# Full attention: steps spread over the beats, queries copied in another order, biases added by TensorE

## The chip, the cores and the metric

The kernel runs on one core of a Trainium2 chip. The metric is the device time of one execution in microseconds (us), the median of several runs. Engines are named as in the profile: PE (TensorE, matrix products), PEld (its weight loads), DVE (VectorE), ACT (ScalarE), POOL (GpSimd) and SP (SyncE, which here only issues transfers, DMAs). They run side by side, each through its own instructions in order, and wait for each other through semaphores.

## The reference, cut to what matters

```
x = L0_attn_x                                             # 16 batches, 512 tokens, 128 channels
x = x + _layernorm(windowed_attention(_layernorm(x)))     # stage 1
x = x + _layernorm(experts(_layernorm(x)))                # stage 2
x = x + _layernorm(full_attention(_layernorm(x)))         # stage 3, the one that is changed
x = x + _layernorm(sine_ffn(_layernorm(x)))               # stage 4

def full_attention(x):            # 16 heads of 8 channels
    qkv = x @ Wqkv + bqkv
    q, k, v = heads(qkv)
    q, k = rope(q), rope(k)
    attn = softmax(q @ k.T * 8 ** -0.5)                   # per batch and head, 512 x 512, no mask
    return merge(attn @ v) @ Wout + bout
```

All of it is computed in fp32. `_layernorm` here has neither gain nor bias.

## The kernel before

The four stages follow one another; `full_attention` is stage 3. Its instructions are recorded under `manual_schedule`: the order of the Python code is the order on each engine. A loop over *beats* writes that order out, 32 beats a batch (`BEATS`). An engine isn't tied to a beat: it goes on as soon as what it waits for is there.

**What each beat does.** `attend(b, k)` multiplies two tiles of scores (keys by queries, `sT`, L1104) and takes their exponentials on ACT (`ex`, L1110). `score(b + 1, k)` multiplies the scores of the next batch in the other order (`s`, L1070), of which DVE takes the greatest of each row (`nm`, L1073), since the softmax subtracts it. Three beats behind, every other beat, `products` multiplies four exponentials by the values (`po`, L1118), and every eighth beat `put_away` copies a finished tile out on ACT (`ou`, L1127) and writes it to DRAM (`heap`, L1128). Two score tiles (`two_banks`, also used by the transposes and projections), three `sT` tiles and one `po` tile fill PSUM.

**Tasks.** What a batch needs once is written as generators that `run_due` advances: `yield n` means that the next step is recorded n beats later. With beats counted from the first attend beat of a batch, modulo 32:

- `arrive` adds the experts' output to x: four gathers `hb` (POOL, L972), four scalings `y` (L978), the sum (L983), a norm, the sum with x (L986).
- `project` (two batches ahead of the attend beats) normalises x (`z_f`), transposes it (L995, ACT copy `zT` L997), multiplies queries and keys (`pqk`, L1002, ACT adds the bias, L1008) and values (`pv`, L1013; DVE adds their bias, L1017). POOL rotates queries and keys (three steps `t` for each half, L1029 to L1032). Each number is cut into a high part (`halves`, DVE, L964) and a rest (POOL, `cut`, L1035), which PE multiplies part by part. SP writes the parts to DRAM (`away`, L1038) and reads them back into the rows that PE needs (`qs`, `ks`, L1056): for each of two units z, queries and keys, two groups r and two parts i, so 16 transfers of 128 KB. Five tiles of queries and five of keys are used in turn.
- `greatest` transposes the greatest of each row (`pm`, L1081), cuts them (L1085) and writes four rows into the queries (L1090).
- `output` reads the heap back (`sc`, `oc`, L1135, L1137), inverts the sums (`rc`, L1140), spreads them over the channels by way of DRAM (`far`, `rb`, L1143, L1144), multiplies (`oT`, POOL, L1147), multiplies by Wout (`pf`, L1151), adds the bias on DVE (`fo`, L1153), normalises, and adds to x (L1156).

The norms (`normed_in`) are statistics on DVE (L182, L183), variance (L187), a power on POOL (L189), a product on DVE (L192) and four scalings on POOL (L197).

The biases of values and output lie in tiles of 128 equal rows:

```
vbias = wp.tile([P, 1, H1 * D1], F32, name="vbias")
bout = wp.tile([P, 1, C], F32, name="bout")
```

Of the kernel before, what the change touches and what calls it, by code (L numbers as in the profile page):

```python
# [20 lines left out]
F32 = mybir.dt.float32  # L21
# [851 lines left out]
def full_attention(net):  # L873
# [20 lines left out]
    with ExitStack() as ctx:  # L894
# [15 lines left out]
        for half in range(2):  # L910
# [8 lines left out]
        vbias = wp.tile([P, 1, H1 * D1], F32, name="vbias")  # L919
        nc.sync.dma_start(  # L920
            out=vbias[:, 0, :], in_=a["L1_attn_bqkv"].rearrange("(o n) -> o n", o=1)[:, 2 * C :].to_broadcast([P, C])
        )
        wo = wp.tile([P, C], F32, name="wo1")
        nc.sync.dma_start(out=wo, in_=a["L1_attn_Wout"])
        bout = wp.tile([P, 1, C], F32, name="bout")
        nc.sync.dma_start(
            out=bout[:, 0, :], in_=a["L1_attn_bout"].rearrange("(o c) -> o c", o=1).to_broadcast([P, C])
        )
        ones_row = net.ones[: H1, :]

        qs = [wp.tile([P, HQ, T], F32R, name=f"qs{i}") for i in range(5)]
        ks = [wp.tile([P, HQ, T], F32R, name=f"ks{i}") for i in range(5)]
        for i in range(5):
# [32 lines left out]
        def arrive(b):  # L966

            xb = net.x[b]
            hb = tok.tile([P, NTB, C], F32, name=f"hb_{b}", tag="fo")
            for j in range(NTB):  # L970
                n = b * NTB + j
                nc.gpsimd.indirect_dma_start(  # L972
                    out=hb[:, j, :], out_offset=None, in_=net.back,
                    in_offset=bass.IndirectOffsetOnAxis(ap=net.slots[:, n : n + 1], axis=0),
                )
            y = tok.tile([P, NTB, C], F32, name=f"y_{b}", tag="z")
            for j in range(NTB):
                nc.gpsimd.tensor_scalar(  # L978
                    y[:, j, :], xb[:, j, :], net.yr[:, b, j : j + 1], net.ynm[:, b, j : j + 1],
                    op0=ALU.mult, op1=ALU.add,  # L980
                )
            yield 11
            nc.gpsimd.tensor_tensor(y, y, hb, ALU.add)  # L983
            yield 4
            yield from normed_in(net, y, f"eo{b}", y)
            nc.gpsimd.tensor_tensor(xb, xb, y, ALU.add)  # L986

        def project(b):

            z = tok.tile([P, NTB, C], F32, name=f"z_f{b}", tag="z")  # L990
            yield from normed_in(net, net.x[b], f"f{b}", z)
            yield 3
# [31 lines left out]
            cuts = []  # L1024
            for half in range(3):

                if half < 2:
                    t1 = rp.tile([P, T], F32, name=f"t1_{b}_{half}", tag=f"t1{half}")
                    nc.gpsimd.tensor_tensor(t1, side[half], rope[:, 0, :], ALU.mult)  # L1029
                    t2 = rp.tile([P, T], F32, name=f"t2_{b}_{half}", tag="t2")  # L1030
                    nc.gpsimd.tensor_tensor(t2, side[1 - half], rope[:, 1, :], ALU.mult)  # L1031
                    nc.gpsimd.tensor_tensor(t1, t1, t2, ALU.add if half else ALU.subtract)  # L1032
                if half:
                    cut, t = cuts[-1]
                    nc.gpsimd.tensor_tensor(cut[:, 1, :], t, cut[:, 0, :], ALU.subtract)  # L1035
                    yield 1
                    for i in range(2):
                        nc.sync.dma_start(  # L1038
                            out=away.rearrange("k r z p h n t -> (k r z) n p h t")[:, :, i, half - 1, :],
                            in_=cut[:, i, :],  # L1040
                        )
                if half < 2:
                    yield 3
                    cut = rp.tile([P, 2, T], F32, name=f"cut_{b}_{half}", tag=f"cut{half}")
                    halves(cut[:, 0, :], t1)
                    cuts.append((cut, t1))
            yield 2
            for z in range(2):
                for kind, to in enumerate((qs, ks)):
                    for r in range(2):  # L1050

                        of = away[kind, r, z].rearrange("p h (d s) t -> p (h d) (s t)", s=HQ)
                        for i in range(2):
                            at = 64 * r + 2 * D1 * i
                            part = of[i : i + 1].to_broadcast([2, D1, HQ * T]) if kind == 0 else of
                            nc.sync.dma_start(  # L1056
                                out=to[(2 * b + z) % 5][at : at + 2 * D1, :, :].bitcast(F32), in_=part
                            )
                yield 3

        def score(b, k):

            z, s, i = k // (HQ * NTB), k // NTB % HQ, k % NTB
            q, kk = qs[(2 * b + z) % 5], ks[(2 * b + z) % 5]
# [10 lines left out]
        def greatest(b, z):  # L1075
# [6 lines left out]
            hi = rp.tile([P, P], F32, name=f"hi_m{b}_{z}", tag="hi_m")  # L1082
            halves(hi[:n], pm[:n, :P])
            lo = rp.tile([P, P], F32, name=f"lo_m{b}_{z}", tag="lo_m")
            nc.vector.tensor_tensor(lo[:n], pm[:n, :P], hi[:n], ALU.subtract)  # L1085
            yield 1
            for r in range(2):
                for j, part in enumerate((hi, lo)):
                    at, of = 64 * r + KR + j, r * HQ * NTB
                    nc.sync.dma_start(  # L1090
                        out=qs[(2 * b + z) % 5][at : at + 1, :, :].bitcast(F32), in_=part[of : of + HQ * NTB, :]
                    )

        def attend(b, k):
# [4 lines left out]
            q, kk = qs[(2 * b + s // HQ) % 5], ks[(2 * b + s // HQ) % 5]  # L1099
# [30 lines left out]
        def output(b):  # L1130
# [14 lines left out]
            yield 6  # L1145
# [4 lines left out]
            for j in range(NTB):  # L1150
                nc.tensor.matmul(pf[:, j, :], lhsT=oT[:, j * P : (j + 1) * P], rhs=wo, start=True, stop=True)  # L1151
            o = tok.tile([P, NTB, C], F32, name=f"fo_{b}", tag="fo")
            nc.vector.tensor_tensor(o, pf, bout.to_broadcast([P, NTB, C]), ALU.add)  # L1153
            yield 1
            yield from normed_in(net, o, f"fo{b}", o)
# [184 lines left out]
```

## Time and profile before

| what | value |
|---|---|
| time, median of 9 runs (lowest to highest) | 2858.79 us (2856.0 to 2874.71) |
| the profiled execution, its own time | 2862.25 us |
| its span, first to last instruction | 2860.5 us |
| mean granted TensorE clock | 0.841 |
| first and last attend beat (sT, L1104) | 1617.0 and 2637.5 us |
| DMA over the attend stage | 28% of 16 engines, 74 GB/s |

In the profile "busy" is time in which an engine works on an instruction. A wait is put down to what ended it. Rows of a timeline give the start, the time, the engine, the line, the operation, the tiles (out<-in) and, in brackets, the idle time before and what ended it. Rows of windows give the stretch, its length, then busy us and instructions of each engine, the granted TensorE clock (1.00 is full speed), the busy share of the DMA engines and GB/s.

### The profile page before, as it was taken

The page shows a single profiled execution, that of the slowest core. Times are in us where ns is not written, and L with a number is a line of the kernel's source. Part 1 is how long each engine was busy: PE and PEld are TensorE (multiplying, and loading weights), DVE is VectorE, ACT ScalarE, POOL GpSimd, SP SyncE. Part 2 cuts the span into 40 slices and gives each one's busy share as a digit, 9 for nine tenths or more (in the row PEclk, how much of TensorE's full clock was granted, in tenths as well). Part 3 has the DMA queues.
Part 4 walks back from the last instruction along what each step waited for, and adds up shares of the span by engine and source line. Part 5 has one row for each costly group of instructions (what it writes and reads, how often), then busy time and mean ns, then how long its engine had stood idle before and what let it go on. Part 6 is the DMA issues. An engine that isn't in the chain of part 4 may idle for free. (4 is left out here: it accounts for less than half of the span.)

```text
span 2860.5 us, 54880 instructions
## 1 busy us (share of the span) xinstructions
PE 2234.4 (78%) x21335; PEld 1263.0 (44%) x21335; DVE 1866.1 (65%) x3711; ACT 1389.2 (49%) x3176; POOL 1410.2 (49%) x1399
## 2 busy tenths in 40 slices
PE   5888988888889882377781698788888888898686
PEld 2555655555556551266770233333333333332354
DVE  3677777777777753856411667677667777771676
ACT  1445554555455450232330156556555555565676
POOL 2556656565665546333324335444444444410598
PEclk8999999999999995566795569889888888876898
DMA  6555555555555531011122223223223323220001
GB/s 173 168 169 151 168 158 161 160 166 160 161 152 164 161 112 51 14 33 39 47 57 48 53 71 84 77 80 85 75 79 83 85 79 80 79 62 29 21 23 33
DMA packets 164289, 275.45 MB, mean 96 GB/s; under 512 B 20419, under 2 KB 64957, under 8 KB 158909
## 3 DMA queue, kind: packets, MB, share of 16 engines
q1 hardware_dynamic: 157696, 259.41, 32.0%
q0 software_dynamic: 4096, 8.40, 1.2%
q10 hardware_dynamic: 2236, 4.12, 0.5%
q8 instruction: 169, 2.77, 0.4%
q14 instruction: 92, 0.75, 0.1%
HBM read 133.55 MB, written 114.03 MB: 87 GB/s over the span
## 5 line engine op out<-in xcount | busy, mean ns | idle before, releaser
L1073 DVE TENSOR_REDUCE nm<-s 128x2 f32<-128x1024 f32 x512 | 612.6, 1220 | 201.3 <-PE s L1070 168.3
L1110 ACT ACTIVATE ex<-sT 128x512 f32<-128x512 f32 x1024 | 537.9, 602 | 394.3 <-PE sT L1104 392.5
L380 POOL TENSOR_TENSOR t<-t,t 128x512 f32<-128x512 f32 x256 | 319.7, 1269 | 379.2 <-DVE t L377 328.4
L431 ACT ACTIVATE pr<-s,nmax 128x96 f32<-128x96 f32 x1024 | 250.8, 355 | 328.3 <-DVE nmax L425 323.2
L1104 PE MATMUL sT<-qs,ks 50*128 50x512 f32 x1024 | 373.2, 548 | 36.0 <-ACT ex L1110 35.9
L1070 PE MATMUL s<-ks,qs 48*128 48x512 f32 x1024 | 315.6, 500 | 89.7 <-DMA ks<-away 64.2
L1118 PE MATMUL po<-ex,vs 128*32 128x512 f32 x2048 | 335.8, 735 | 0.0
L1104 PEld LDWEIGHTS sT<-qs,ks 50*128 50x128 f32 x1024 | 150.7, 211 | 384.2 <-ACT ex L1110 252.3
L371 PE MATMUL pq<-xnT,wqk 128*128 128x512 f32 x512 | 264.4, 640 | 24.6 <-DVE t L377 23.4
L375 DVE TENSOR_TENSOR t<-pq,rope 128x1024 f32<-128x1024 f32 x128 | 156.5, 1223 | 167.8 <-DMA far<-t 89.5
L443 POOL TENSOR_TENSOR pr<-pr,rc 128x768 f32<-128x768 f32 x128 | 187.9, 1468 | 54.7 <-DVE rc L442 45.8
L1070 PEld LDWEIGHTS s<-ks,qs 48*128 48x128 f32 x1024 | 137.9, 220 | 129.8 <-issue 74.6
L456 ACT COPY prT<-pt 96x512 f32<-96x512 f32 x256 | 138.7, 602 | 111.5 <-PE pt L454 111.5
L392 PE MATMUL pv<-wv,xnT 128*128 128x512 f32 x256 | 151.5, 677 | 29.6 <-ACT v_odd L396 29.6
L377 DVE TENSOR_TENSOR t<-pq,rope 128x1024 f32<-128x1024 f32 x128 | 155.3, 1213 | 0.0
L454 PE MATMUL pt<-ident,pr 64*96 64x64 f32 x2048 | 84.6, 223 | 83.0 <-POOL pr L443 82.8
L425 DVE TENSOR_REDUCE nmax<-s 128x8 f32<-128x768 f32 x128 | 118.1, 923 | 46.4 <-PE s L420 46.3
L485 PE MATMUL pf<-wo,oT 128*128 128x128 f32 x1024 | 129.8, 281 | 15.1 <-ACT v_odd L396 15.1
L371 PEld LDWEIGHTS pq<-xnT,wqk 128*128 128x128 f32 x512 | 90.1, 196 | 112.3 <-issue 95.1
L485 PEld LDWEIGHTS pf<-wo,oT 128*128 128x128 f32 x1024 | 123.1, 194 | 32.8 <-ACT v_odd L396 17.3
L471 PEld LDWEIGHTS po<-prT,v_even 96*64 96x64 f32 x2048 | 103.3, 137 | 75.5 <-issue 39.4
L471 PE MATMUL po<-prT,v_even 96*64 96x64 f32 x2048 | 132.6, 228 | 0.7 <-ACT prT L456 0.7
(258 smaller groups left out, 4113.0 us busy)
## 6 DMA issues: line engine op xcount, KB each, us to landing
far<-t SPq DMA_DIRECT2D x256, 256.0 KB
kT<-far SPq DMA_DIRECT2D x64, 512.0 KB
qT<-far SPq DMA_DIRECT2D x64, 512.0 KB
away<-cut SPq DMA_DIRECT2D x64, 256.0 KB
qs<-away SPq DMA_DIRECT2D x128, 128.0 KB
ks<-away SPq DMA_DIRECT2D x128, 128.0 KB
heap<-ou SPq DMA_DIRECT2D x64, 256.0 KB
v_even<-v_odd SPq DMA_DIRECT2D x32, 384.0 KB
```

The costliest lines, as they stand in the source:

```text
L371: nc.tensor.matmul(ps[:, s], lhsT=wqk[:, kind, 2 * half + g, s, :], rhs=xnT[b][:, :T], start=True, stop=True)
L375: nc.vector.tensor_tensor(t1, ps, rope[:, 0:1, :].to_broadcast([P, 2, T]), ALU.mult)
L380: nc.gpsimd.tensor_tensor(t1[:, s], t1[:, s], t2[:, 1 - s], ALU.add if s else ALU.subtract)
L431: nc.scalar.activation(pr[:, r, j, :], s[:, r, j * KW : (j + 1) * KW], AF.Exp, bias=nmax[:, r, j : j + 1])
L443: nc.gpsimd.tensor_tensor(pr, pr, per_token(rc, KW), ALU.mult)
L471: nc.tensor.matmul(po[D0 * r : D0 * r + D0, t : t + 64], lhsT=v[:KW, j, at : at + D0], rhs=prT[:KW, c, r, j, :], start=True, stop=True,)
L485: nc.tensor.matmul(pf[:, i, :], lhsT=o[:, p, j * P : (j + 1) * P], rhs=wo[:, NP * half + p, :], start=(p == 0), stop=(p == NP - 1),)
L1070: nc.tensor.matmul(ps[:, r, :], lhsT=q[rows, s, i * P : (i + 1) * P], rhs=kk[rows, s, :], start=True, stop=True)
L1073: nc.vector.tensor_reduce(nms[b, z][:, :, s, i], ps, AX.X, ALU.max, negate=True)
L1104: nc.tensor.matmul(t, lhsT=kk[rows, s % HQ, i * P : (i + 1) * P], rhs=q[rows, s % HQ, :], start=True, stop=True)
L1110: nc.scalar.activation(e, st[r], AF.Exp, scale=SCALE1)
L1118: nc.tensor.matmul(outs[-1][PADH * j : PADH * (j + 1), :], lhsT=vs[b % 3][:, i, VW * (NJ * g + j) : VW * (NJ * g + j) + PADH], rhs=weights ...
```

## The change

It touches the full attention alone (and one helper, by an argument that is zero elsewhere). The steps of the tasks get other beats; the scores of a batch start 24 beats before its attend beats, not 32; projections and arrivals start earlier; each step by its beat, modulo 32:

| step | before | after |
|---|---|---|
| gathers hb | 10 (all four) | 7, 8, 9, 10 |
| scalings y; sum with hb | 10; 21 | 11; 16 |
| norm of arrive: statistics; power; scalings; x | 25, 26; 26; 28; 28 | 18, 19; 20; 22; 23 |
| norm of project: statistics; power; z_f | 0, 1; 1; 3 | 22, 23; 24; 26 |
| transposes; pqk; pv | 6; 8; 10 | 30; 0; 2 |
| rotation, first and second half | 10; 13 | 2; 5 |
| halves; cut | 13, 17; 13, 17 | 7, 10; 8, 11 |
| away | 14, 18 | 10, 13 |
| qs and ks of unit 0; of unit 1 | 20; 23 | 15; 20 |
| maxima of unit 0 (pm; rows) | 17; 18 | 25; 26 |
| maxima of unit 1 (pm; rows) | 1; 2 | 9; 10 |
| oT; pf | 14; 16 | 15; 17 |
| norm of output: statistics; power; scalings; x | 17, 18; 18; 20; 20 | 20, 21; 22; 24; 26 |

From the transposes to the units' copies, `project` stands in the batch two before its own in both kernels, with its norm in the batch three before in the changed one; its first score is at beat 0 of the next batch before, and at beat 8 after. Before the first attend beat the order changes too: arrival 1 comes before projection 0, and projection 1 before the first score.

The copies of queries: one transfer of 256 KB for each unit and group, in place of two of 128 KB, with 16 outer rows; the rows of queries and keys stand in another order, which leaves the sums alone. The biases of values and output are single rows, added by a further matmul with a row of ones; ACT then copies the PSUM tile, where DVE added the bias. Both parts of the maxima lie in one tile.

```diff
-def normed_in(net, x4, name, out, scale=None, mul=1.0, add=LN_EPS):
+def normed_in(net, x4, name, out, scale=None, mul=1.0, add=LN_EPS, apart=0):
...
     nc.vector.tensor_scalar(v, mv[:, :, 1], mul, add, op0=ALU.mult, op1=ALU.add)
+    if apart:
+        yield apart
     r = net.small.tile([P, k], F32, name=f"r_{name}", tag="cr")
...
+        vbias = wp.tile([1, C], F32, name="vbias")
+        bout = wp.tile([1, C], F32, name="bout")
...
                 nc.tensor.matmul(
                     pv[:, i, :], lhsT=zT[:, i * P : (i + 1) * P], rhs=raw[:, 2].rearrange("c h d -> c (h d)"),
-                    start=True, stop=True,
+                    start=True, stop=False,
                 )
-            nc.vector.tensor_tensor(
+                nc.tensor.matmul(pv[:, i, :], lhsT=net.ones[:1, :], rhs=vbias, start=False, stop=True)
+            nc.scalar.copy(
                 vs[b % 3][:, :, : VW * H1].rearrange("p i (h d) -> p i h d", d=VW)[:, :, :, :D1],
                 pv.rearrange("p i (h d) -> p i h d", d=D1),
-                vbias.to_broadcast([P, NTB, C]).rearrange("p i (h d) -> p i h d", d=D1),
-                ALU.add,
             )
...
                         of = away[kind, r, z].rearrange("p h (d s) t -> p (h d) (s t)", s=HQ)
+                        rows = to[(2 * b + z) % NH].bitcast(F32)
+                        if kind == 0:
+                            nc.sync.dma_start(
+                                out=rows[64 * r : 64 * r + 4 * D1, :, :],
+                                in_=of.rearrange("p d x -> (p d) x").unsqueeze(1).to_broadcast([2 * D1, 2, HQ * T]),
+                            )
+                            continue
                         for i in range(2):
                             at = 64 * r + 2 * D1 * i
-                            part = of[i : i + 1].to_broadcast([2, D1, HQ * T]) if kind == 0 else of
                             nc.sync.dma_start(
-                                out=to[(2 * b + z) % 5][at : at + 2 * D1, :, :].bitcast(F32), in_=part
+                                out=rows[at : at + 2 * D1, :, :], in_=of.rearrange("p d x -> d p x")
                             )
-                yield 3
+                yield 5
...
-                nc.tensor.matmul(pf[:, j, :], lhsT=oT[:, j * P : (j + 1) * P], rhs=wo, start=True, stop=True)
+                nc.tensor.matmul(pf[:, j, :], lhsT=oT[:, j * P : (j + 1) * P], rhs=wo, start=True, stop=False)
+                nc.tensor.matmul(pf[:, j, :], lhsT=net.ones[:1, :], rhs=bout, start=False, stop=True)
             o = tok.tile([P, NTB, C], F32, name=f"fo_{b}", tag="fo")
-            nc.vector.tensor_tensor(o, pf, bout.to_broadcast([P, NTB, C]), ALU.add)
-            yield 1
-            yield from normed_in(net, o, f"fo{b}", o)
+            nc.scalar.copy(o, pf)
+            yield 3
+            yield from normed_in(net, o, f"fo{b}", o, apart=1)
+            yield 2
...
+        LEAD = 24
+        arrivals = {(n - 4) * BEATS + 7: n for n in range(3, B)} | {-121: 0, -117: 1, -79: 2}
+        projections = {(n - 3) * BEATS + 22: n for n in range(1, B)} | {-100: 0}
         with tc.manual_schedule():
-            for beat in range(-3 * BEATS, (B + 1) * BEATS):
+            for beat in range(-4 * BEATS, (B + 1) * BEATS):
                 b, k = divmod(beat, BEATS)
+                sb, sk = divmod(beat + LEAD, BEATS)
...
-                if 0 <= b + 1 < B:
-                    score(b + 1, k)
-                    if k % (BEATS // 2) == BEATS // 2 - 1:
-                        tasks.append([beat, greatest(b + 1, 2 * k // BEATS)])
+                if 0 <= sb < B:
+                    score(sb, sk)
+                    if sk % (BEATS // 2) == BEATS // 2 - 1:
+                        tasks.append([beat, greatest(sb, 2 * sk // BEATS)])
...
-                if k == BEATS - 22 and b + 3 < B:
-                    tasks.append([beat, arrive(b + 3)])
-                if k == 0 and 0 <= b + 2 < B:
-                    tasks.append([beat, project(b + 2)])
+                if beat in arrivals:
+                    tasks.append([beat, arrive(arrivals[beat])])
+                if beat in projections:
+                    tasks.append([beat, project(projections[beat])])
```

More of the change, by code (lines that the diff above doesn't have):

```diff
@@ L918, in full_attention @@
                         )
[L919 to L922, printed above, removed]
+        vbias = wp.tile([1, C], F32, name="vbias")
+        nc.sync.dma_start(out=vbias, in_=a["L1_attn_bqkv"].rearrange("(o n) -> o n", o=1)[:, 2 * C :])
         wo = wp.tile([P, C], F32, name="wo1")
         nc.sync.dma_start(out=wo, in_=a["L1_attn_Wout"])
[L925 to L928, printed above, removed]
+        bout = wp.tile([1, C], F32, name="bout")
+        nc.sync.dma_start(out=bout, in_=a["L1_attn_bout"].rearrange("(o c) -> o c", o=1))
         ones_row = net.ones[: H1, :]
-        qs = [wp.tile([P, HQ, T], F32R, name=f"qs{i}") for i in range(5)]
-        ks = [wp.tile([P, HQ, T], F32R, name=f"ks{i}") for i in range(5)]
-        for i in range(5):
+        NH = 5
+        qs = [wp.tile([P, HQ, T], F32R, name=f"qs{i}") for i in range(NH)]
+        ks = [wp.tile([P, HQ, T], F32R, name=f"ks{i}") for i in range(NH)]
+        for i in range(NH):
             for r in range(2):
@@ L975, in arrive @@
                 )
+                yield 1
             y = tok.tile([P, NTB, C], F32, name=f"y_{b}", tag="z")
@@ L981, in arrive @@
                 )
-            yield 11
+            yield 5
             nc.gpsimd.tensor_tensor(y, y, hb, ALU.add)
-            yield 4
-            yield from normed_in(net, y, f"eo{b}", y)
+            yield 2
+            yield from normed_in(net, y, f"eo{b}", y, apart=1)
+            yield 1
             nc.gpsimd.tensor_tensor(xb, xb, y, ALU.add)
@@ L990, in project @@
             z = tok.tile([P, NTB, C], F32, name=f"z_f{b}", tag="z")
-            yield from normed_in(net, net.x[b], f"f{b}", z)
-            yield 3
+            yield from normed_in(net, net.x[b], f"f{b}", z, apart=1)
+            yield 4
             pz = two_banks(f"tp_f{b}")[:, 0, :]
@@ L1022, in project @@
             )
             away = dp.tile([2, 2, 2, 2, 2, HD * HQ, T], F32, name=f"away_{b}", tag="away")
[L1024 to L1035, printed above, removed]
-                    yield 1
[L1037 to L1046, printed above, removed]
@@ new lines, in project @@
+            ts = []
+            for half in range(2):
+                t1 = rp.tile([P, T], F32, name=f"t1_{b}_{half}", tag=f"t1{half}")
+                nc.gpsimd.tensor_tensor(t1, side[half], rope[:, 0, :], ALU.mult)
+                t2 = rp.tile([P, T], F32, name=f"t2_{b}_{half}", tag="t2")
+                nc.gpsimd.tensor_tensor(t2, side[1 - half], rope[:, 1, :], ALU.mult)
+                nc.gpsimd.tensor_tensor(t1, t1, t2, ALU.add if half else ALU.subtract)
+                ts.append(t1)
+                yield 3 - half
@@ new lines, in project @@
+            for half in range(2):
+                cut = rp.tile([P, 2, T], F32, name=f"cut_{b}_{half}", tag=f"cut{half}")
+                halves(cut[:, 0, :], ts[half])
+                yield 1
+                nc.gpsimd.tensor_tensor(cut[:, 1, :], ts[half], cut[:, 0, :], ALU.subtract)
+                yield 2
+                for i in range(2):
+                    nc.sync.dma_start(
+                        out=away.rearrange("k r z p h n t -> (k r z) n p h t")[:, :, i, half, :], in_=cut[:, i, :]
+                    )
@@ L1081, in greatest @@
             nc.tensor.transpose(pm[:n, :P], nm.rearrange("p r s i -> p (r s i)"), net.ident)
[L1082 to L1085, printed above, removed]
+            parts = rp.tile([P, P], F32, name=f"m{b}_{z}", tag="m")
+            halves(parts[:n], pm[:n, :P])
+            nc.vector.tensor_tensor(parts[64 : 64 + n], pm[:n, :P], parts[:n], ALU.subtract)
             yield 1
             for r in range(2):
-                for j, part in enumerate((hi, lo)):
-                    at, of = 64 * r + KR + j, r * HQ * NTB
+                for j in range(2):
+                    at, of = 64 * r + KR + j, 64 * j + r * HQ * NTB
                     nc.sync.dma_start(
-                        out=qs[(2 * b + z) % 5][at : at + 1, :, :].bitcast(F32), in_=part[of : of + HQ * NTB, :]
+                        out=qs[(2 * b + z) % NH][at : at + 1, :, :].bitcast(F32), in_=parts[of : of + HQ * NTB, :]
                     )
@@ L1098, in attend @@
             s = NJ // 2 * g + j
[L1099 removed]
+            q, kk = qs[(2 * b + s // HQ) % NH], ks[(2 * b + s // HQ) % NH]
             st = []
@@ L1144, in output @@
             nc.sync.dma_start(out=rb, in_=far.to_broadcast([H1, D1, T]))
-            yield 6
+            yield 7
             oT = op.tile([P, T], F32, name=f"oT1_{b}", tag="oT")
```

8 lines of the change are left out of this document (5 added, 3 removed).

## Prediction

> **What bounds the kernel now.** I read the page first, then the full attention by windows and by waits, then the timelines around its longest waits. The page:
>
> ```profile
> PE 2234.4 (78%) x21335; PEld 1263.0 (44%) x21335; DVE 1866.1 (65%) x3711; ACT 1389.2 (49%) x3176; POOL 1410.2 (49%) x1399
> PEclk8999999999999995566795569889888888876898
> ```
>
> TensorE is the busiest engine, and from the 15th slice on its granted clock is below full. The change touches only the full attention, whose attend beats run from 1617.0 (first sT, L1104) to 2638.9. The windows of that stage, then of three batches in it (us; busy us of PE, PEld, DVE, ACT, POOL; clock):
>
> ```profile
> 1617.00:2638.90 1021.90, 881.27 (x4397) 327.09 (x4397) 694.39 (x1036) 592.53 (x1129) 401.18 (x484) 0.82 0.28 74
> 1691.40:1756.90 65.50, 57.30 (x282) 21.40 (x280) 46.32 (x71) 37.32 (x72) 28.93 (x35) 0.79 0.24 69
> 1818.40:1879.60 61.20, 50.70 (x282) 19.30 (x282) 45.99 (x71) 37.13 (x72) 28.93 (x35) 0.92 0.32 85
> ```
>
> A batch takes 1021.9 / 16 = 63.9 us. DVE, ACT and POOL do the same work in both batches shown (46, 37, 29 us), and PE's busy time grows as its clock falls. No other engine fills a batch: PE, its clock and what it waits for set the pace. The windows of line 1104 alone (two matmuls a beat) give the pace at each clock:
>
> ```profile
> 1663.60:1690.50 26.90, 12.24 (x24) 5.37 (x24) 0.50 0.45 100
> 1824.00:1847.50 23.50, 8.90 (x28) 3.54 (x28) 1.00 0.29 94
> 1858.70:1879.00 20.30, 9.70 (x28) 3.89 (x28) 1.00 0.37 90
> ```
>
> At half clock a beat takes 26.9 / 12 = 2.24 us, at full clock 20.3 / 14 = 1.45 us, and 23.5 / 14 where the transposes and products of `project` lie among the beats. A mean clock of 0.82 means 36% of the stage at half clock. PE's waits in the stage and the two that recur in every batch:
>
> ```profile
> PE pf L1151 <- POOL oT L1147: 66.5, 12, 6.0
> PE s L1070 <- DMA ks<-away: 26.9, 15, 5.7
> 1792.52 2.08 PE L1151 MATMUL pf<-wo,oT 128*128 128x128 f32 x8 [5.28 <-POOL oT L1147]
> 1758.64 1.17 PE L1070 MATMUL s<-ks,qs 48*128 48x512 f32 x2 [1.82 <-DMA ks<-away]
> ```
>
> Beat 16 waits some 5.5 us for oT, beat 0 some 1.8 us for the queries and keys to be scored. After each the clock drops: 0.50 from 1759.3 to 1762.7 after the second one shown, and in other batches for 6.8 to 20 us. A wait of 1.13 us at 2520.7 was followed by 34 us at 0.50, in which PE was busy 34.1 of 34.1 us; gaps of 0.55 to 0.78 us (1838.6, 1777.3) were followed by none. So what must go are idle stretches from about 1.1 us up.
>
> Why oT is late, on POOL's timeline:
>
> ```profile
> 1775.54 1.27 POOL L1029 TENSOR_TENSOR t<-qk,rope 128x512 f32<-128x512 f32 x1 [6.80 <-ACT qk L1008]
> ...
> 1779.55 1.07 POOL L972 DMA_INDIRECT hb<-back,slots  x1 [0.16 <-issue]
> ...
> 1784.41 1.81 POOL L978 TENSOR_SCALAR y<-x,yr,ynm 128x128 f32<-128x128 f32 x4
> ...
> 1789.98 1.26 POOL L1035 TENSOR_TENSOR cut<-t,cut 128x512 f32<-128x512 f32 x1
> 1791.20 1.26 POOL L1147 TENSOR_TENSOR oT<-oc,rb 128x512 f32<-128x512 f32 x1
> ```
>
> POOL works without a gap from 1775.5 to 1792.5 on seven rotary and cutting steps (beats 10 and 13), four gathers and four scalings (beat 10); oT queues behind them. Batch 13, which has no arrival, has no such wait (pf began at 2496.27 without one). Why the queries are late, on SP's timeline:
>
> ```profile
> 1811.36 8.00 SPq L1056 DMA_DIRECT2D qs<-away  x4
> 1819.43 1.77 SPq L1056 DMA_DIRECT2D ks<-away  x4
> ```
>
> Four issues for queries take 8 us, each waiting for an earlier query transfer to land (2.45 us apart); four for keys take 1.8 us, and the score waits for them behind the queries.
>
> **The change, part by part.** *POOL spread.* From beat 2 POOL now does six rotary steps (6 x 1.26), four gathers (4 x 1.25), two cuts (2 x 1.26) and four scalings (1.8): 16.9 us. Starting when ACT's qk is out, some 3 us into the batch, and waiting about 2 us for DVE's halves of beat 7, it is through near 22 us. oT's input rb leaves SP after rc of beat 8 (about 17 us) and the 1.5 us that SP waited between far and rb (1776.99, 1778.46), so lands by about 22. oT ends near 23.5; PE comes to beat 17 at 17 x 1.45 + 3 = 27.6. The wait goes with 4 us to spare; if that cover fails it costs 5.5 us again and the clock.
>
> *Projection earlier.* The query transfers of unit 0 are issued 25 beats before their first score instead of 12, 36 us against 17. The wait of beat 0 goes even if the transfers gained nothing. The new form halves the query issues; SP has 32 DMAs a batch, not 36.
>
> The Trainium skill ("DMA: Bandwidth & Descriptors", section on why a DMA increments its semaphore by 16) states that the slowest dimension decides over how many of the 16 engines a transfer goes. By that rule queries go from 2 engines to 16, but keys, whose source now has 8 outer rows, from 16 to 8: it speaks against that part. The 8.0 and 1.8 us rows above agree with it for before; by the rule or without it the sum here is the same, as 36 us cover either.
>
> *Maxima later.* LEAD 24 puts the maxima of unit 1 on SP at beat 10, needed at beat 16. Ahead of them on SP stand rb, heap and two away, behind POOL's cut; four issues at 0.6 us. From rb at 19 us: heap 0.4, away 1.2, maxima 2.4, landing about 2, so 25 us against beat 16 at 26. That is thin.
>
> *Biases.* Eight matmuls a batch of two passes: in place of "pv" and "pf" with 8 passes there are 16 each. pf's 8 passes took 1.09 us at full clock (2496.27 to the next start at 2497.36). No one-row matmul is in the trace: from 0 (hidden under PE's waits for DVE) to 0.38 us each (the first, isolated pass of pv, 1839.15); I take the neighbours' 0.12: 16 x 0.12 = 1.9 us. DVE loses two additions of 0.69 us, ACT gains two copies of 0.59 us (rows of vs, fo and zT); ACT's 37 us leave room. Each copy waits for its matmuls, and behind it the next exponentials wait 0.6 us, inside PE's present gaps; PE would notice only through its three sT buffers.
>
> *DVE.* The statistics of three norms (four pairs of about 0.4 and two steps of 0.16 each, 1.9) now lie in beats 18 to 23: 5.7 us beside 6 x 1.22 of maxima, 12.9; PE has 6 x 1.45 + 2 of pf, 10.7. That overhang of some 2 us is mostly buffered by two score tiles; between 0 and 2, I take 0.4.
>
> *A batch then.* 32 x 1.45 = 46.4; project's extra 23.5 - 14 x 1.45 = 3.2; pf 1.1; biases 1.9; DVE 0.4: 53 us at full clock.
>
> *Start.* Arrival 1 now comes before projection 0, and projection 1 before the first score. POOL's work from the first gather (1503.57) to z of batch 1 is three arrivals of 12.1, one projection of 12.9 and 2.8: 52; with waits for DVE and ACT like those in its rows (2.0 x 2, 5.5) about 62, and 5.5 more to qk: first score at 1571.5, against 1565.8. Then 24 beats at (1617.0 - 1565.8) / 32 = 1.6 us: 1610, 7 earlier. The bounds are 1600 and 1625.
>
> *Sum.* Start 1610; batch 0, half clock for its first 3 beats, 55; batches 1 to 13 at 53, 689; batch 14 without projection 49; batch 15: 8 beats at 1.45, 10 alone at 1.30, 14 alone at 2.1 (as batch 15 did, half clock from its 12th beat), pf: 55. That ends at 2458; the tail of 2860.5 - 2638.9 = 222 stays: 2680, 1.8 around it as before (2862.25 against 2860.5): 2682. The median of the runs lies 3.5 below the profiled one: **2678 us**.
>
> The Trainium skill ("TensorE: Matmul & The Clock Gate", Part 1) says one busy window of 3.4 us brings full clock back. By this rule a batch would lose its two waits, 7.3 us, and twice 3.4 us at half clock, 2.4 us: less 1.9 for the biases that is 7.8 us, 117 in 15 batches, and with the start 7 the estimate would be 2735. The 34 us at 0.50 with PE fully busy contradict the rule, so the rows decide.
>
> **The rivals.** *oT stays late* (POOL's crowd is only moved): against it, batch 13; for it, rb or halves may hold POOL. Price: 5.5 us plus 6.8 us at half clock (2.5) a batch, 14 x 8 = 112: 2790. *The clock falls in beats 18 to 26*, where DVE holds PE: 9 beats of 0.8 us, 14 x 7 = 98: 2776. Against it, PE would still be busy 10.7 of 12.9 us there.
>
> *The maxima come late at beat 16*, the one that ends slower. If they land over 1.1 us after PE is there, it idles, and the clock stays low until the transposes of beat 30: 1.5 + 15 x 0.79 = 13.4 us on top of 53 is 66.4, above today's 63.9: 15 x 13.4 = 201, so 2879. For it, the 1 us of slack; against it, pf's matmuls stand at beat 17, and after today's late pf the clock came back within 6.8 us.
>
> *The change does not do what it says*: the order of the instructions on each engine shows the steps moved as described, and nothing before the attention; I give this nothing.
>
> **How the numbers follow.** Forecast 0.64, oT late 0.12, clock in the DVE stretch 0.14, maxima late 0.08, no net effect 0.02. The forecast's own range: start -10 to +15, biases -1.9 to +4 a batch (-27 to +60): 2640 to 2750. Reaching to the two mild rivals: 2640 to 2795. A change under 0.3%, 8.6 us, can't be told from none. Faster 0.90, same 0.02, slower 0.08.
>
> **What would show it.** Right: no wait of pf for oT or of s for ks over 1 us, clock near 1.0 from batch 1 to 14, batches of 51 to 55 us, first sT near 1610. Wrong: sT of beat 16 waiting for a DMA; half clock for ten beats in a batch; pf still in the waits; a 16-pass pf far above 2.2 us.

## The result, and the profile after

The changed kernel takes 3080.29 us (median of 20 runs, 3036.7 to 3110.28), the kernel before 2854.07 us in the same comparison: ratio 1.0758, 95% interval 1.0729 to 1.0786. It is slower by 7.6%, where 2678 us and faster was forecast. A ratio compares, of each kernel, only the executions within 1.5% of its fastest, so it can differ a little from the ratio of the medians. The profiled execution took 3068.59 us, with a span of 3066.8 us.

The page of the changed kernel, PE's busy time and the granted clock by slices:

```profile
PE 2570.8 (84%) x21591; PEld 1395.1 (45%) x21591; DVE 1863.7 (61%) x3679; ACT 1406.4 (46%) x3208; POOL 1411.7 (46%) x1399
PEclk8999999999999955778855755555755557575799
```

TensorE has 256 more matmul records than before, 1.2% of them, and 336 us more busy time. Nothing of that size was added; the slices with 5 say where it comes from. The windows of the attend stage, first sT (line 1107 here) to the last (start:end, length; busy us of PE, PEld, DVE, ACT, POOL; clock):

```profile
1614.60:2840.70 1226.10, 1205.11 (x4641) 453.54 (x4641) 694.78 (x994) 605.36 (x1157) 386.53 (x462) 0.60 0.22 61
```

The stage is 204.2 us longer than before (1021.9), the whole span 206.3. PE is busy 1205.1 of 1226.1 us, so it waits less than before, and its mean clock went from 0.82 to 0.60. PE's waits in the stage, all that the view lists:

```profile
PE sT L1107 <- ACT ex L1113: 12.2, 44, 0.8
PE s L1073 <- ACT zT L999: 3.3, 9, 0.7
PE sT L1107 <- DMA qs<-m: 3.3, 2, 1.8
PE pqk L1004 <- DVE nm L1076: 0.5, 1, 0.5
```

pf no longer waits for oT (66.5 us before), s no longer for ks (26.9 us). The waits that the change was to take away are gone, and the clock is lower all the same. The timeline of the values' product in one batch shows what TensorE does just before the clock falls (start, us, engine, line, operation, tiles, xcount):

```profile
1849.60 0.49 PE L1015 MATMUL pv<-raw,zT 128*128 128x128 f32 x2
1850.02 0.48 PE L1019 MATMUL pv<-vbias,ones 1*128 1x128 f32 x2
1850.43 0.49 PE L1015 MATMUL pv<-raw,zT 128*128 128x128 f32 x2
1850.85 0.48 PE L1019 MATMUL pv<-vbias,ones 1*128 1x128 f32 x2
...
1852.93 0.51 PE L1107 MATMUL sT<-qs,ks 50*128 50x512 f32 x2
```

The 16 passes take 1852.93 - 1849.60 = 3.33 us, 0.21 us each; without biases the 8 passes of this block took 1.09 us at full clock. The windows of that block, of the stretch after it, and of a pf block with the stretch after it:

```profile
1849.60:1852.93 3.33, 3.33 (x18) 2.36 (x17) 1.23 (x1) 1.25 (x3) 3.25 (x3) 1.00 0.21 79
1853.80:1861.00 7.20, 7.20 (x29) 2.35 (x21) 3.59 (x3) 3.17 (x7) 2.78 (x3) 0.50 0.17 46
2733.86:2737.18 3.32, 3.32 (x20) 2.36 (x16) 0.34 (x1) 0.00 (x0) 0.00 (x0) 1.00 0.00 0
2737.90:2843.70 105.80, 101.74 (x344) 32.40 (x341) 32.03 (x47) 51.50 (x100) 9.35 (x13) 0.50 0.07 22
```

In both blocks PE is busy without a gap at full clock, and within 1 us of their ends the clock is 0.50: the second time for 105.8 us, through the rest of the stage, in which PE was busy 101.7. A *fall* is from here on a change of the granted clock from 1.00 to 0.50. The traces show no other values, and in the attend stages the times between two changes are whole multiples of 3.41 us, so the 3.41 us ahead of a fall are the window to look at. Of the 19 falls in the stage, 17 follow a window with five to eight one-row passes and no idle time. The other two follow the wait for the maxima at beat 16 (1.78 and 1.48 us). In the kernel before, every fall followed a window in which PE was busy for at most 2.45 of 3.41 us.

### The profile page after: what moved, and what is told of

It reads as the page before. It is cut to its first block, busy times and chain, and to the rows that moved or that the text cites. A ratio compares the mean times of both kernels' runs of the same rounds, so it can differ in the third digit from the quotient of the medians.

```text
span 3066.8 us, 55235 instructions
## 1 busy us (share of the span) xinstructions
PE 2570.8 (84%) x21591; PEld 1395.1 (45%) x21591; DVE 1863.7 (61%) x3679; ACT 1406.4 (46%) x3208; POOL 1411.7 (46%) x1399
## 4 chain that ended last, share of the span: by engine, by line
PE 38%; POOL 4%; DVE 4%; ACT 3%; issue 1%; DMA 1%; POOLq 0%; ACTq 0%; DVEq 0%; SPq 0%
PE po L1121 13%; PE sT L1107 12%; PE s L1073 6%; DVE nm L1076 1%; PE pqk L1004 1%; PE pf L1154 1%; PE pf L1155 1%; ACT ex L1113 1%; PE pv L1019 1%; PE pv L1015 1%; POOL go L199 1%; POOL turns L1277 1%; POOL x L1300 1%; DVE whole L1281 1%; DMA qs<-m 1%
## 5 line engine op out<-in xcount | busy, mean ns | idle before, releaser
L1076 DVE TENSOR_REDUCE nm<-s 128x2 f32<-128x1024 f32 x512 | 621.5, 1220 | 450.0 <-PE s L1073 443.1
L1107 PE MATMUL sT<-qs,ks 50*128 50x512 f32 x1024 | 470.3, 684 | 17.6 <-ACT ex L1113 12.2
L1121 PE MATMUL po<-ex,vs 128*32 128x512 f32 x2048 | 441.9, 952 | 0.0
L1073 PE MATMUL s<-ks,qs 48*128 48x512 f32 x1024 | 411.6, 611 | 18.3 <-DVE nm L1076 14.7
L1107 PEld LDWEIGHTS sT<-qs,ks 50*128 50x128 f32 x1024 | 200.1, 267 | 486.3 <-issue 286.8
L1073 PEld LDWEIGHTS s<-ks,qs 48*128 48x128 f32 x1024 | 183.3, 285 | 35.6 <-DVE nm L1076 26.1
```

The lines of the kernel that those rows point to most:

```text
L1073: nc.tensor.matmul(ps[:, r, :], lhsT=q[rows, s, i * P : (i + 1) * P], rhs=kk[rows, s, :], start=True, stop=True)
L1076: nc.vector.tensor_reduce(nms[b, z][:, :, s, i], ps, AX.X, ALU.max, negate=True)
L1107: nc.tensor.matmul(t, lhsT=kk[rows, s % HQ, i * P : (i + 1) * P], rhs=q[rows, s % HQ, :], start=True, stop=True)
L1121: nc.tensor.matmul(outs[-1][PADH * j : PADH * (j + 1), :], lhsT=vs[b % 3][:, i, VW * (NJ * g + j) : VW * (NJ * g + j) + PADH], rhs=weights ...
```

## The experiments

Two theories were put first. **A**: a matmul over one row leaves the array nearly empty, so the clock gate takes a window full of them for an idle one. **B**: the harm is in the alternation of two sets of weights, whatever their rows. A third, **C**: the new places of the steps (LEAD, the longer pauses) are to blame, the biases are not. The runs fall into three comparisons, in which the kernel before took 2870.66, 2856.46 and 2852.19 us; each ratio is to the one of its own comparison.

**Biases back on VectorE, all else as changed.**

```diff
-  nc.tensor.matmul(pv[:, i, :], lhsT=net.ones[:1, :], rhs=vbias, start=False, stop=True)
-  nc.scalar.copy(vs..., pv...)
+  nc.vector.tensor_tensor(vs..., pv..., vbias..., ALU.add)      # and the same for pf, bout
```

> The changed kernel with the biases added by DVE again, as before; everything else stays changed. Theory A (the one-row matmuls let the clock fall: 16 of the 19 falls in the changed kernel's attend beats follow a window with 5 to 8 one-row passes and no idle time): the falls after pv and pf vanish, the stage is at full clock except after a late maxima row at beat 16; 2680 to 2850 us, mean clock over the attend stage above 0.8. Theory B (it is the alternation of one-row and full weights, 0.21 us a pass in place of 0.11, whatever the rows): the same as A. Theory C (the new places of the steps pull the clock down, the biases cost only their own 5 us a batch): about 3080 - 15 x 5 = 3000 us, clock in the stage still near 0.6.

Measured: 2768.33 us (2755.52 to 2783.59), ratio to the kernel before 0.9635 (0.9567 to 0.9702). The biases' form alone turns a gain of 3.6% into a loss of 7.6%; C falls. Stage and waits of this kernel:

```profile
1626.50:2559.20 932.70, 862.14 (x4409) 319.38 (x4409) 711.62 (x1023) 590.89 (x1128) 387.63 (x462) 0.85 0.29 80
PE s L1078 <- DVE nm L1081: 16.1, 27, 1.0
PE sT L1112 <- DMA qs<-m: 11.8, 13, 2.1
```

The stage lost 293.4 us against the changed kernel. What is left to explain is a batch of 58.3 us (932.7 / 16) where 53 was forecast. The clock still falls 21 times. Seven falls come 28 to 29 us into a batch, after waits of 0.83 to 2.08 us for the maxima at beat 16; one comes in the last batch, and the other 13 come 38 us or later into a batch, where PE waits for VectorE's score maxima. Six of these follow a single wait of 0.67 or 0.68 us, with the rest of the window almost all busy. One such wait and its window, after which the clock fell at 1797.42:

```profile
1796.37 0.50 PE L1078 MATMUL s<-ks,qs 48*128 48x512 f32 x2 [0.67 <-DVE nm L1081]
1794.01:1797.42 3.41, 2.71 (x20) 1.01 (x16) 3.23 (x12) 2.06 (x4) 0.40 (x2) 1.00 0.85 169
```

**The kernel before, with only the one-row biases and the copies by ScalarE.**

```diff
-  nc.vector.tensor_tensor(vs..., pv..., vbias..., ALU.add)
+  nc.tensor.matmul(pv[:, i, :], lhsT=net.ones[:1, :], rhs=vbias, start=False, stop=True)
+  nc.scalar.copy(vs..., pv...)                                   # and the same for pf, bout
```

> The kernel before with one part of the change alone: biases by one-row matmuls and copies on ACT, all steps at their old beats. Theories A and B: each pv at beat 10 and pf at beat 16 is followed by half clock; the attend stage is at half clock 70 to 80% of its time and the kernel takes 3000 to 3150 us. Theory C: only the time of the passes is added, 15 x 5 us: about 2930 us.

Measured: 2957.11 us (2944.79 to 2973.33), ratio 1.0326 (1.0257 to 1.0396). Same direction, less than expected: the time lies between C's 2930 us and the 3000 from which A and B start, and doesn't decide between them. The clock does: in the stage it went from 0.82 to 0.77, and 15 of its 27 falls now follow windows with six to eight one-row passes and less than 0.1 us without work. That the loss is smaller because the kernel before already ran much of its stage at half clock is likely, and was not tested.

**The bias matmuls over all 128 rows.**

```diff
-  vbias = wp.tile([1, C], F32)        # the bias, one row
+  vbias = wp.tile([P, C], F32)        # the bias / 128 in every row
-  nc.tensor.matmul(pv[:, i, :], lhsT=net.ones[:1, :], rhs=vbias, ...)
+  nc.tensor.matmul(pv[:, i, :], lhsT=net.ones, rhs=vbias, ...)   # and the same for pf
```

> The changed kernel with as many bias matmuls, but each over 128 rows (a tile of ones times 128 rows of a 128th of the bias) in place of one. Theory A (rows count): clock as in the kernel with DVE biases, plus 16 passes of 0.11 us a batch: within 60 us of that kernel, 2700 to 2880. Theory B (alternation of weights counts, or ACT's copies): passes still 0.21 us and the clock still falls after pv and pf: 3040 to 3100. Theory C: 3000 to 3080.

Measured: 2789.02 us (2769.22 to 2797.09), ratio 0.973 (0.9671 to 0.979). The number of matmuls and their alternation are those of the changed kernel; only the rows differ. Timeline of the values' block, and windows of the stage and of this block with 1.5 us behind it:

```profile
1872.46 0.49 PE L1019 MATMUL pv<-raw,zT 128*128 128x128 f32 x2
1872.78 0.39 PE L1023 MATMUL pv<-vbias,ones 128*128 128x128 f32 x2
1873.01 0.39 PE L1019 MATMUL pv<-raw,zT 128*128 128x128 f32 x2
...
1874.44 0.50 PE L1111 MATMUL sT<-qs,ks 50*128 50x512 f32 x2
```
```profile
1626.00:2546.00 920.00, 827.95 (x4641) 326.55 (x4642) 692.99 (x994) 603.12 (x1157) 387.68 (x462) 0.92 0.29 81
1872.46:1875.90 3.44, 3.44 (x29) 2.31 (x28) 1.90 (x2) 2.57 (x6) 3.36 (x4) 1.00 0.23 81
```

Sixteen passes take 1874.44 - 1872.46 = 1.98 us, about 0.12 each, the price that the prediction put on them, and no fall of the clock follows any of these blocks. B falls. A bias matmul on TensorE isn't what hurts; one with few rows is.

**One one-row matmul of 512 columns for each tile, ahead of the four products.**

```diff
+  nc.tensor.matmul(pv, lhsT=net.ones[:1, :], rhs=vbias.unsqueeze(1).to_broadcast([1, NTB, C]), start=True, stop=False)
   for i in range(NTB):
-      nc.tensor.matmul(pv[:, i, :], lhsT=zT..., rhs=raw..., start=True, stop=False)
-      nc.tensor.matmul(pv[:, i, :], lhsT=net.ones[:1, :], rhs=vbias, start=False, stop=True)
+      nc.tensor.matmul(pv[:, i, :], lhsT=zT..., rhs=raw..., start=False, stop=(i == NTB - 1))
```

> The changed kernel with one bias matmul of one row over all 512 columns of the tile, ahead of the four products, in place of four of 128 columns between them. The one-row passes go from 8 of 0.21 us, alternating, to 2 of about 0.22 to 0.43 us in one piece. Theory A: less than 1.1 us of nearly empty array, so falls after pv and pf become rare: 2700 to 2900 us. Theory B: no alternation, so the same. Theory C: about 3000 us. If a single one-row matmul is enough for a fall, the time stays above 3000 too and the half-clock stretches still begin right after pv and pf.

Measured: 2831.37 us (2788.99 to 2860.48, the widest spread here), ratio 0.9785 (0.968 to 0.9889). The block takes 2.14 us, and a single fall follows bias passes with no other gap beside them. Two readings stay open after this: few one-row columns (A), or few changes between one row and 128 (call it **D**, since such changes cost time, 3.33 against 1.98 us for 16 passes, and that time might be an idle array).

**32 rows.** Against the changed kernel:

```diff
-  vbias = wp.tile([1, C], F32)
+  vbias = wp.tile([32, C], F32)       # the bias / 32 in every row
-  nc.tensor.matmul(pv[:, i, :], lhsT=net.ones[:1, :], rhs=vbias, ...)
+  nc.tensor.matmul(pv[:, i, :], lhsT=net.ones[:32, :], rhs=vbias, ...)   # and the same for pf
```

> The changed kernel with each bias matmul over 32 rows (ones times a 32nd of the bias) in place of 1: between the changed kernel (one row, 3080 us) and e3 (128 rows, 2789). If the clock's gate weighs rows in proportion, 32 rows are a quarter of the array: most falls after pv and pf stay, 2950 to 3080. If any matmul that fills one group of 32 rows counts, 2770 to 2830. If weights that differ in rows can't be loaded beside each other (0.21 us a pass), that stays at 32 rows too, and shows apart from the clock.

Measured: 3035.84 us (3022.97 to 3054.06), ratio 1.0623 (1.0545 to 1.07). The blocks take 3.33 us again, and 19 of 20 falls follow them. So 32 rows hardly help, under A and D alike.

**64 rows**, the same with 64, and **one-row passes in a row**: the one-row matmul of 512 columns twice, with half the bias each, ahead of the products. The first keeps the changes of row count and doubles the rows; the second doubles the one-row time and has one change.

```diff
-  vbias = wp.tile([32, C], F32); lhsT=net.ones[:32, :]
+  vbias = wp.tile([64, C], F32); lhsT=net.ones[:64, :]           # the bias / 64; the same for pf
```
```diff
-  nc.tensor.matmul(pv, lhsT=net.ones[:1, :], rhs=vbias.unsqueeze(1)..., start=True, stop=False)
+  for half in range(2):               # vbias halved once at the start; the same for pf
+      nc.tensor.matmul(pv, lhsT=net.ones[:1, :], rhs=vbias.unsqueeze(1)..., start=half == 0, stop=False)
```

> The changed kernel with each bias matmul over 64 rows (ones x bias/64). Passes of 1 and of 32 rows that alternate with 128-row passes followed each other 0.21 us apart (16 passes in 3.33 us), passes of 128 rows 0.11 us apart (1.98 us). Two readings are left. Rows weigh (A): a 64-row pass counts half, the window's loss halves, few falls follow the bias blocks, 2790 to 2850. Each switch between a pass of fewer rows and one of 128 empties the array for 0.10 us (D): the block still takes 3.33 us, falls follow it as they do with 32 rows, 3010 to 3080.

> The kernel with one one-row matmul of 512 columns ahead of the four products (2831), but that matmul is there twice with half the bias each, so 4 one-row passes of some 0.43 us stand back to back with one change of row count, about 1.7 us of one-row work in a block of 3.0 us. Rows weigh (A): half a window is one-row work, the clock falls after nearly every block, 3000 to 3100. Only the switches count (D): no more falls than with one such matmul, 2830 plus 14 x 2 x 0.9 = 2855, 2840 to 2880.

Measured: 64 rows 2903.92 us (2881.71 to 2912.3), ratio 1.0195 (1.0156 to 1.0235). A block takes 3.16 us, so the changes cost nearly what they did, and yet the clock stays up. A window with all eight 64-row passes of a values' block, and the one behind it:

```profile
2165.30:2168.70 3.40, 3.40 (x20) 2.47 (x20) 1.23 (x1) 1.31 (x3) 3.32 (x3) 1.00 0.20 77
2168.70:2172.10 3.40, 3.19 (x25) 1.10 (x25) 2.33 (x2) 2.93 (x6) 3.15 (x4) 1.00 0.31 87
```

Of 15 full-clock windows with six or more 64-row passes, in which PE is busy for 3.3 us or more, none is followed by a fall. With one row (the changed kernel) all 16 of such windows are, with 32 rows all 18, with 128 rows none of 22. Eleven of the 14 falls with 64 rows come where passes of a pf block and a wait for ScalarE's exponentials lie in the same window, 0.5 to 1.3 us of it; the time is 54 us above A's band, and further still from D's. As a wait of 0.67 us was enough in the first experiment without any bias matmul, these falls hardly tell what 64 rows weigh.

One-row passes in a row: 2954.88 us (2941.2 to 2981.63), ratio 1.0387 (1.0317 to 1.0457). That is 45 us below A's band, but D allowed 2880 at most. Eighteen of its 23 falls follow windows without a gap in which all or most of the one-row passes lie. Such a window and the values' block in it:

```profile
2443.60:2447.00 3.40, 3.40 (x15) 1.51 (x12) 1.73 (x2) 2.37 (x5) 3.32 (x4) 1.00 0.23 84
2445.69 1.02 PE L1017 MATMUL pv<-vbias,ones 1*128 1x512 f32 x2
2446.64 1.78 PE L1022 MATMUL pv<-raw,zT 128*128 128x128 f32 x8
```

The eight passes of the products took 1.78 us, where they took 1.09 at full clock: the clock fell at 2447.0, amid them. D falls, and A stands in kind, though its times were off in both runs: PE's busy time is not what the gate goes by; how many rows the passes fill counts. In windows like these 1 and 32 rows act like idle time, 64 and 128 like work. The runs don't give an exact law, and as all these matmuls have weights of 128 columns, they don't tell rows from the filled area of the array.

**What else costs the forecast's batch.** With the biases on VectorE, LEAD 28 gives the maxima four more beats:

```diff
-        LEAD = 24
+        LEAD = 28
```

> DVE biases as in e1, and the scores of a batch 28 beats ahead of its attend beats in place of 24: the maxima of unit 1 go out at beat 6, ahead of far and rb on SP, and are needed at beat 16. In e1 six batches wait 0.93 to 2.08 us at beat 16 for them. Theory A1 (these waits still pull the clock down): they vanish, and with them 1.3 us and a stretch of 3 to 20 us at half clock in about six batches: 2715 to 2755 us against 2768. Theory A2 (what is left in e1 is DVE's crowd in beats 18 to 25, where PE waits about 1 us twice for nm): no more than 15 us better, or none, since the maxima's transposes only move into another crowded beat: 2750 to 2780.

Measured: 2799.48 us (2793.24 to 2806.88), ratio 0.9805 (0.9751 to 0.9859). The waits for the maxima are gone and the time went up, out of the bands of both theories: now twelve batches of 16 drop to half clock some 39 us in, where the maxima of unit 0 fall among the norms' statistics on VectorE. So the second cause weighs more. Next, the arrivals ten beats later, which takes one norm away from there:

```diff
-        arrivals = {(n - 4) * BEATS + 7: n for n in range(3, B)} | {-121: 0, -117: 1, -79: 2}
+        arrivals = {(n - 4) * BEATS + 17: n for n in range(3, B)} | {-121: 0, -117: 1, -79: 2}
```

> e5 with the arrivals of batches 3 and on ten beats later (17 in place of 7), so that the statistics of their norm leave beats 18 and 19 for 28 and 29. Theory A1: as e5 within 10 us. Theory A2 (DVE's crowd of three norms makes PE wait for nm, and the clock falls): both remaining causes are gone, batches of 52 to 54 us at full clock: 2660 to 2710. If gathers at beats 17 to 20 on POOL collide with oT, pf would wait for oT again.

Measured: 2731.85 us (2728.02 to 2744.0), ratio 0.9572 (0.9515 to 0.9628); better by 68 us, 22 short of the expectation. Ten of its 16 falls still come 38 to 40 us into a batch. VectorE's timeline there, and the windows before and after that fall:

```profile
1760.15 0.28 DVE L182 BATCH_NORM_STATS2 st_fo<-fo 128x6 f32<-128x128 f32 x1
...
1761.29 0.28 DVE L968 TENSOR_SCALAR m<-pm 32x128 int32<-32x128 int32 x1
1761.60 0.28 DVE L1093 TENSOR_TENSOR m<-pm,m 32x128 f32<-32x128 f32 x1
```
```profile
1759.30:1762.70 3.40, 2.05 (x13) 0.96 (x16) 3.19 (x9) 2.17 (x4) 1.04 (x1) 1.00 0.84 202
1762.80:1786.50 23.70, 23.70 (x83) 8.24 (x76) 17.17 (x32) 10.66 (x20) 8.81 (x15) 0.50 0.13 40
```

VectorE is busy 3.19 of 3.40 us, PE 2.05; the maxima (line 1093) stand behind the output norm's statistics, and the next scores behind the maxima. PE is then busy for 23.7 of 23.7 us at half clock. The dense biases in the same order, that is, the kernel of the 128-row biases with the same two edits:

```diff
-        LEAD = 24
+        LEAD = 28
-        arrivals = {(n - 4) * BEATS + 7: n ...
+        arrivals = {(n - 4) * BEATS + 17: n ...
```

> e6 with the biases by matmuls of 128 rows in place of DVE. Theory A (a full array keeps the clock): within 25 us of e6 on either side; PE has 16 passes of 0.11 us more in a batch (1.8 us, 28 us in all), DVE 1.4 us less. If ACT's copies or the weight changes hurt, over 2740.

Measured: 2764.56 us (2751.88 to 2773.72), ratio 0.9683 (0.9622 to 0.9745): no fall follows the biases, but this is 33 us slower than additions on VectorE, more than the 25 us of theory A. The passes' own time at full clock, 2 x (1.98 - 1.09) us a batch or some 28 us in all, would be most of it; that was not tested by itself. Taking the biases from VectorE gained nothing.

**LEAD 24 with the late arrivals**, and **the output norm's statistics six beats later**, each against the kernel of 2731.85 us:

```diff
-        LEAD = 28
+        LEAD = 24
```
```diff
             nc.vector.tensor_tensor(o, pf, bout.to_broadcast([P, NTB, C]), ALU.add)
-            yield 3
+            yield 9
-            for beat in range(-4 * BEATS, (B + 1) * BEATS):
+            for beat in range(-4 * BEATS, (B + 1) * BEATS + 8):
```

> The fastest version with LEAD 24 in place of 28, which parts LEAD from the arrivals' place. If the late maxima of unit 1 come of LEAD (10 beats for them), TensorE waits at beat 16 again and the time is 2750 to 2790; if the arrivals at beat 7 made them late, by their gathers and heap issues on the queues, no such wait comes and the time is 2700 to 2735.

> The fastest version so far (biases by VectorE, LEAD 28, arrivals at 17; 2732) with the statistics of the output's norm six beats later, off the beat in which the maxima of unit 0 are taken. If that crowd on VectorE makes the clock fall (11 of 16 falls there, 38.5 us into the batch, cold for some 15 us each), these go and the time is 2680 to 2715. Rival: the statistics only meet those of the projection's norm, the fall moves to beats 26 to 30, and the time stays at 2720 to 2745.

Measured: LEAD 24 gives 2730.77 us (2713.72 to 2752.49), ratio 0.9558 (0.9498 to 0.9619), as fast as LEAD 28. PE waits for the maxima 7 times, 6.5 us in all, where it waited 13 times, 11.8 us, with early arrivals: both LEAD and the arrivals make them late, and neither expectation holds alone. VectorE's waits, now 41 to 52 us into the batch, took up the rest. The later statistics give **2682.31 us** (2673.49 to 2686.84), ratio 0.9414 (0.9385 to 0.9442), the fastest kernel of all. Its stage, a window of 53 us in it, and its longest wait for DVE:

```profile
1612.80:2450.00 837.20, 761.76 (x4401) 288.37 (x4401) 696.84 (x1020) 586.13 (x1128) 389.79 (x467) 0.97 0.32 89
1770.00:1823.00 53.00, 47.95 (x284) 18.53 (x284) 47.96 (x72) 37.52 (x74) 29.01 (x35) 1.00 0.35 98
PE tp_f L1001 <- DVE nm L1081: 17.8, 13, 1.5
```

The clock is 0.97, eight batches of 16 take 53.4 to 53.6 us, and no fall is left 38 us into a batch. What is left are waits of tp_f for VectorE at 51 to 53 us, with 3.4 to 6.8 us at half clock after them, in eight batches.

## Why the prediction was wrong, point by point

**The step that failed is the biases.** The prediction wrote 16 x 0.12 = 1.9 us a batch and 0 to 0.38 us for each pass. Measured at full clock: 3.33 - 1.09 = 2.24 us a block, two blocks a batch, 4.5 us, or 2.24 / 8 = 0.28 us for each added pass; that is within the bounds. The loss is the other part, which no term stood for: the prediction let the clock stay up through these passes, and they pulled it down. Against VectorE's additions the stage is 293.4 us longer, 18.3 us a batch, and 18.3 - 4.5 leaves about 14 us a batch, lost while the stage's mean clock is 0.60 and not 0.85. The range reached +4 us a batch for unknown costs of the biases. The row that it leaned on, neighbours of 128 rows, was not a near one.

**The criterion for the clock was incomplete.** "Idle stretches from about 1.1 us up" was read from a stage in which every matmul is over 48 rows or more. The runs show three corrections: gaps add up within a window of some 3.4 us (falls followed 0.44 + 0.91 us), a single gap of 0.67 us can be enough (first experiment), and passes with 1 or 32 rows count like gaps. What the prediction took from the rows against the Trainium skill holds: "TensorE: Matmul & The Clock Gate", Part 1, has the gate follow how busy the engine has been and one busy window restore full clock. Here 105.8 us at 0.50 with PE busy 101.7 speak against the second once more, and a fall after 3.40 of 3.40 us that the records call busy speaks against the first.

**Waits of pf and s: right.** Both are gone. **POOL's spread and the earlier projection: right**, at no visible price.

**Maxima at beat 16, the rival that was to end slower: it happens, but is not why the kernel is slower.** The changed kernel has it twice, in batches that reached beat 16 at full clock; with the clock kept (biases on VectorE) 13 times, 11.8 us in all. Its price was put too high: six of those seven falls lasted 3.4 us, not until beat 30. The chance of 0.08 for slower was thus given to a mechanism that did not produce it.

**DVE in beats 18 to 26: underweighted.** The forecast charged 0.4 us; the rival at 0.14 charged 7 us a batch and 2776 us. With the biases on VectorE 2768 us was measured, with such a fall in 13 batches of 16, at beats 24 to 28; with biases over 128 rows, which give VectorE no addition, 2789 us and such a fall in 11. Had the biases been harmless, this rival would have been the nearest, though the falls after the maxima are part of these times too.

**First sT at 1610, the tail of 222: right.** First sT came at 1614.6, the tail took 3066.8 - 2840.7 = 226.1. **The batch of 53 us** is not the changed kernel's (1226.1 / 16 = 76.6); it is seen only in the version with all three causes taken away: 53.5 us, stage 837 against 848 forecast, 2682 against 2678. That the time agrees to 4 us is partly luck: that version has no bias matmuls, and the forecast's batch without its 1.9 us for them would be 51. The sum of work was near; that the clock would stay up was wrong.

**Small slips.** On the page the clock drops in the 16th slice, not the 15th, and 5.7 + 6 x 1.22 is 13.0; nothing rests on either.

## What to carry to other kernels

Do not fold a bias into a product by a one-row matmul in a stretch that lives on a full TensorE clock: spread the bias over 128 rows, or leave it to an engine with room. When a kernel's pace hangs on the granted clock, ask of every added matmul not only how long it takes but how many rows it fills, and add up the gaps within the 3.4 us between two possible changes of the clock instead of judging each alone. A wait that has been removed uncovers the next one: order the small steps of an engine that paces the beats (here VectorE's norm statistics and maxima) so that no two of them meet.

## What the runs showed of the hardware

- The granted clock fell after 3.41 us in which PE's records show (almost) no idle time, when much of that time was passes of few rows. Of the full-clock windows with six to eight bias passes and PE busy for 3.3 us or more, 16 of 16 (changed kernel) and 15 of 15 (kernel before with one-row biases) were followed by a fall with 1 row, 18 of 18 with 32 rows, none of 15 with 64 rows, none of 22 and none of 17 in the two kernels with 128 rows.
- Without such passes, falls followed windows in which PE was busy for 2.73 us or less; a window with 2.01 us (the version of 2732 us) was not followed by one, so the busy time alone doesn't decide.
- A pass of 1, 32 or 64 rows that alternates with passes of 128 rows costs more than a pass of 128: 16 passes of 128 columns took 3.33, 3.33, 3.16 and 1.98 us with 1, 32, 64 and 128 rows.
- Half clock mostly lasts while only the beats' own matmuls run (sT over 50 rows and s over 48, in each half of the array, po over 128 rows with weights of 32 columns): in the changed kernel 190 of 194 such windows at half clock were followed by another. Of the windows at half clock that hold products of 128 rows by 512 columns (pqk), 11 of 13 were followed by full clock in the version with LEAD 28 and early arrivals, 8 of 9 in the fastest version, 4 of 9 in the changed kernel. That fits the weight of rows; no run tried it by itself.
